# Four-layer graph network on one core: table parts and a convolution cut into steps, and the queues around layer 2's experts reordered

## The chip, the core and the metric

The kernel runs on one core of a Trainium2 chip, as one launch. The core has five engines that run on their own and meet only through semaphores: TensorE (PE, matrix products, its weight loads shown apart as PEld), VectorE (DVE), ScalarE (ACT), GpSimd (POOL) and SyncE (SP, which here only issues DMAs). Each takes its instructions strictly in its own order. The metric is the device time of one execution in microseconds, as the median of several runs; lower is better. Everything is computed in 32-bit floating point.

## The reference

1250 nodes with 512 features and 21250 edges pass through four layers. Every layer adds a graph convolution and an attention to the residual stream, and then a feed-forward part:

```
x = x + graph_l(norm(x)) + mix_l(norm(x));  x = x + ffn_l(norm(x))
layer 0: three GATv2 layers, h = relu(norm(segment_sum(xl[src] * alpha) + b + h))
         xl = h @ Wl[k], xr = h @ Wr[k]; alpha = segment softmax of leaky_relu(xl[src]+xr[dst]+ef) @ att[k]
layer 1: dense GAT and global attention; ffn: top-2 of experts plus shared part
layer 2: EGC: bases = x @ W_bases; agg = normalised neighbour sum of bases;
         conv[n,h,f] = sum_b w[n,h,b] * agg[n,b,f];  mix: linear attention
         ffn: xt = transpose(x); logits = conv1(gelu(conv3(xt)));  top 2 of 10 experts, elu
              sh = conv1(silu(conv9(xt)));  z = x + experts + sh;  norm(z) * g + b
layer 3: GCN: dinv = rsqrt(deg); out = segment_sum(h[row] * dinv[row]*ew*dinv[col]) + b
         mix: linear attention with q scaled;  ffn: top 2 of 32 experts with capacity
```

`conv9` and `conv3` are one-dimensional convolutions over the 1250 nodes, 9 and 3 taps wide.

## The kernel before

Nodes are cut into 10 tiles of 128 rows (`NT`), the last holding 98. Matrix products work on 128x128 weights and up to 512 columns. `psum(mm, tp, more)` deals out the eight PSUM banks by use; `evac` copies a PSUM result out, alternately on ACT and on DVE. The order of instructions on each engine is made by a scheduler at build time, from priorities in program order and modelled durations; inside `manual_schedule(engines=...)` the named engines keep the order in which the code is written. `experts` does that for SP. Stages run in this order (times are those of the profile):

- **Layer 0**, its ffn included, to 2240: preparation and linear attention to 320, then to 1620 the three GATv2 layers (`gatv2_fast`), edge tile by edge tile: rows of a left table are gathered by POOL (L231), PE expands the right table with one-hot matrices (L1280, L1281), DVE makes sum, and the score product `junk` (L1293, L1296), PE sums the weighted rows (L1347). While layer k runs, `gat_tables` makes the tables of layer k+1 (or, in `gat_first`, the first ones): for each node tile eight steps, four accumulating products for `wl` and four for `wr`, one step at a time between edge tiles, in a single PSUM bank, `tab`. With the fourth product of a half come ACT's copy (L1174, L1182) and a DVE operation on the same bank (L1176 `junk`, L1183).
- **Layer 1**, 2240 to 3160: dense attention, then experts from 2985 to 3103 and their tail.
- **Layer 2's attention** (`layer2_attn`), 3160 to 3397. From 3240 a loop over the ten tiles: a row of the count matrix `ct` is cast to `cs` by `evac`, ten products (L2571) give `y`, DVE scales it to `ag` (L2577), and for four bases b DVE makes `m = w[:, :, b] * ag[b]` (L2585), which POOL adds up. Linear attention (`q`, L748 to L817) runs between.
- **Layer 2's ffn** (`layer2_ffn`), 3397 to 3811. The normalised rows are transposed into `xp`; three sums and differences of even and odd columns (`form`, L2687) let a convolution be done with fewer products. Each weight `piece` is loaded in three DMAs and gets three sums on POOL (L2624 to L2626); up to five pieces are in flight. The 3-tap convolution gives the router's logits (3445 to 3513). Then follow, one after the other, the 9-tap convolution in two halves f of three pieces each (to 3622), the `second` products (L2780, L2782, to 3651), and 29 expert tiles (to 3811). For each, SP loads 256 KB of tokens `xe` and 1 MB of weights `w`, four buffers of each, three tiles ahead; PE transposes, multiplies (L2338), DVE and ACT make the elu (L2788 to L2792), PE multiplies again (L2343). The vector `be` is added to x by POOL during the transposes.
- **Layer 2's tail and the head of layer 3**, 3811 to 3919. `tail_steps` chains, tile by tile: two gathers of expert rows on POOL (`g`), z sums on DVE (L2807), row norm (ACT L2816, POOL L2817 with `ga`), the addition to x, the norm `xn` (L222), and the transposition `xnT` (PE L160 and `evac`). `layer3_attn` starts by making the degree scales `dinv` (L2837 to L2844) and writing them to memory and reading them back as `dinvb`, blocks of 107 nodes in columns (L2858 to L2863), 4 bytes at a time; it loads four 1 MB weights, scales `wq` on POOL (L762), and makes `o` on DVE (L2851), which ACT's queue writes out.
- **Layer 3**: GCN loop 3919 to 4225, then 32 experts to 4584.

Of the kernel before, what the change touches and what calls it, by code (L numbers as in the profile page):

```python
# [57 lines left out]
class Net:  # L58
# [675 lines left out]
    def linear_attention_steps(self, xn, xT, w_qkv, w_out, b_out, qscale, finish, added=None,  # L734
# [15 lines left out]
        with self.tc.tile_pool(name="la", bufs=1) as p, \  # L750
# [7 lines left out]
            for half in range(2):  # L758
                if half:
                    wq = self.weight(w_qkv[:, 0:D], 4, D)  # L760
                    if qscale != 1.0:
                        nc.gpsimd.tensor_scalar(wq, wq, qscale, None, op0=ALU.mult)  # L762
# [391 lines left out]
    def gat_tables(self, L, p, t, xT, bank):  # L1154
# [7 lines left out]
        def product(name, c):  # L1162
            def f():
# [4 lines left out]
                if c == 3:  # L1168
                    (left if name == "wl" else right)(d[name])
            return f  # L1170

        def left(m):
            o = p.tile([128, D + 1], F32, tag="tlo", name="tlo")
            nc.scalar.copy(o[:, :D], m)  # L1174
# [5 lines left out]
        def right(m):  # L1180
            o = p.tile([128, 2, D], F32R, tag="tro", name="tro")
            nc.scalar.copy(o[:, 0, :], m)  # L1182
# [3 lines left out]
        return [product(name, c) for name in ("wl", "wr") for c in range(4)]  # L1186
# [314 lines left out]
    def run(self, fast):  # L1501
# [4 lines left out]
        with self.tc.tile_pool(name="arm", bufs=1) as self.arm:  # L1506
# [23 lines left out]
            with self.psum():  # L1530
                self.layer2_ffn()
# [35 lines left out]
    def gat_first(self, pv, xtab):  # L1567
        nc, I = self.nc, self.I
        L = self.gat_vectors(0, pv)
        with self.tc.tile_pool(name="l0", bufs=1) as p, \  # L1570
# [3 lines left out]
            with self.tc.tile_pool(name="edge", bufs=1, side="right") as pe, \  # L1574
# [19 lines left out]
                def steps():  # L1594
                    for t in range(NT):
                        for i, f in enumerate(self.gat_tables(
# [3 lines left out]
                            if i % 4 == 3:  # L1600
# [710 lines left out]
    def experts(self, table, n, rowI, act):  # L2311
# [5 lines left out]
        with self.tc.tile_pool(name="ex", bufs=2) as p, \  # L2317
                self.tc.manual_schedule(engines={mybir.EngineType.SP}):
            def load(i):
                xe = p.tile([128, D], F32, tag="xe", name="xe", bufs=4)  # L2320
                nc.sync.dma_start(xe, self.rin[i * 128:(i + 1) * 128, :])
                row = nc.sync.value_load(rowI[0:1, i:i + 1], min_val=0, max_val=(n - 1) * 128)
                w = p.tile([128, 2050], F32, tag="w", name="w", bufs=4)
                nc.sync.dma_start(w, table[bass.ds(row, 128), :])
                return xe, w

            ahead = [load(i) for i in range(3)]
            for i in range(ntiles):
                xe, w = ahead.pop(0)
                if i + 3 < ntiles:  # L2330
                    ahead.append(load(i + 3))
# [16 lines left out]
                nc.scalar.dma_start(self.rout[i * 128:(i + 1) * 128, :], o)  # L2348

# [6 lines left out]
    def tail_steps(self, xn, xnT):  # L2356
# [5 lines left out]
        def turn(t):  # L2362
            self.transpose_tile(xnT[:, :, t * 128:(t + 1) * 128], xn[:, t, :])
# [11 lines left out]
        def need(t):  # L2375
            for u in range(t - n if t == 0 else t, t + 1):
                for i, f in enumerate(steps):
                    if 0 <= u + n - i < NT:
                        f(u + n - i)
# [104 lines left out]
    def layer2_attn(self):  # L2484
        nc, I = self.nc, self.I
        added = self.both_added()
        with self.tc.tile_pool(name="l2", bufs=1) as p:
# [17 lines left out]
            with self.tc.tile_pool(name="egc", bufs=2) as tmp, \  # L2505
# [55 lines left out]
                for t in range(NT):  # L2561
# [5 lines left out]
                    self.evac(cs, ct)  # L2567
# [604 lines left out]
```

## Time and profile before

| | |
|---|---|
| median of 3 runs | 4537.75 us (4534.72 to 4541.73) |
| profiled execution, its own time | 4585.94 us |
| its span | 4584.0 us |
| mean granted TensorE clock in it | 0.931 |
| PE, DVE, ACT, POOL busy, share of the span | 86%, 59%, 33%, 31% |
| GAT loop, 400 to 700: PE busy per 100 us | 89.25, 92.72, 93.80 |
| 3360 to 3440: PE busy per 20 us | 15.15, 9.87, 9.43, 12.82 |
| experts of layer 1, 2985 to 3103: PE busy, DMA | 112.59 of 118, 332 GB/s |
| experts of layer 2, 3651 to 3811: PE busy, DMA | 127.91 of 160, 252 GB/s |
| tail, 3800 to 3880: PE busy per 20 us | 9.52, 0.00, 12.41, 9.87 |

The profile records one execution, and every time below is on its clock, from the start of its span. An instruction is named by engine, source line and tile: `DVE m L2585` writes the tile m on VectorE. A busy time counts execution alone; what an engine waits for is put down to the instruction that released it last. The granted clock is the share of full speed that PE was given in a window. The profiled execution takes 48 us longer than the median.

### The profile page before, as it was taken

The page shows a single profiled execution, that of the slowest core. Times are in us where ns is not written, and L with a number is a line of the kernel's source. Part 1 is how long each engine was busy: PE and PEld are TensorE (multiplying, and loading weights), DVE is VectorE, ACT ScalarE, POOL GpSimd, SP SyncE. Part 2 cuts the span into 40 slices and gives each one's busy share as a digit, 9 for nine tenths or more (in the row PEclk, how much of TensorE's full clock was granted, in tenths as well). Part 3 has the DMA queues.
Part 4 walks back from the last instruction along what each step waited for, and adds up shares of the span by engine and source line. Part 5 has one row for each costly group of instructions (what it writes and reads, how often), then busy time and mean ns, then how long its engine had stood idle before and what let it go on. Part 6 is the DMA issues. An engine that isn't in the chain of part 4 may idle for free. (4 is left out here: it accounts for less than half of the span.)

```text
span 4584.0 us, 49281 instructions
## 1 busy us (share of the span) xinstructions
PE 3946.8 (86%) x15451; PEld 2434.6 (53%) x15466; DVE 2706.4 (59%) x6387; ACT 1502.9 (33%) x2738; POOL 1402.3 (31%) x1339
## 2 busy tenths in 40 slices
PE   6988998899788866799999999997969975898796
PEld 3435554555354444444788876564546552454474
DVE  5358784878398865533796767314692136587301
ACT  2213332334133354110364446122221122455121
POOL 2027662766366501102000000103253003676101
PEclk9989998999899978899999999999989997997798
DMA  6446664666466423401421110392012185565695
GB/s 221 150 123 199 184 188 138 192 185 187 130 180 189 145 66 105 121 18 59 147 68 42 44 41 21 140 336 80 12 54 71 69 282 154 162 205 170 244 338 188
DMA packets 283000, 647.57 MB, mean 141 GB/s; under 512 B 61673, under 2 KB 108905, under 8 KB 267322
## 3 DMA queue, kind: packets, MB, share of 16 engines
q1 hardware_dynamic: 169290, 357.13, 23.5%
q0 software_dynamic: 73088, 234.75, 17.9%
q10 hardware_dynamic: 40352, 52.44, 3.4%
q8 instruction: 127, 2.08, 0.2%
q14 instruction: 143, 1.17, 0.1%
HBM read 528.87 MB, written 120.65 MB: 142 GB/s over the span
## 5 line engine op out<-in xcount | busy, mean ns | idle before, releaser
L231 POOL DMA_INDIRECT xl<-xl,srcI x564 | 606.6, 1075 | 309.4 <-issue 137.4
L1347 PE MATMUL more<-xl,wT 128*128 128x512 f32 x1128 | 578.5, 600 | 26.8 <-ACT wT L1337 25.3
L1280 PE MATMUL mm<-hl,oh 121*128 121x512 f32 x564 | 419.6, 744 | 89.7 <-DVE s L1293 29.7
L1293 DVE TENSOR_TENSOR s<-xl,mm 128x512 f32<-128x512 f32 x534 | 355.0, 680 | 99.9 <-PE mm L1281 42.3
L1296 DVE SCALAR_TENSOR_TENSOR junk<-s,att 128x512 f32<-128x512 f32 x534 | 409.8, 767 | 6.2
L2099 PE MATMUL more<-hh,e 128*128 128x259 f32 x1600 | 384.0, 386 | 11.1 <-ACT o L2042 8.9
L2099 PEld LDWEIGHTS more<-hh,e 128*128 128x128 f32 x1600 | 295.0, 191 | 75.6 <-issue 16.0
L171 PE MATMUL mm<-w,xnT 128*128 128x512 f32 x640 | 307.7, 620 | 13.7 <-DVE xnT L136 5.3
L231 POOL DMA_INDIRECT g<-routed_out,getI x60 | 64.7, 1079 | 676.7 <-DMA routed_out<-o 490.0
L231 POOL DMA_INDIRECT hs<-gcn_h,srcI x188 | 215.5, 1146 | 96.5 <-issue 35.9
L1347 PEld LDWEIGHTS more<-xl,wT 128*128 128x128 f32 x1128 | 196.5, 192 | 86.2 <-ACT wT L1337 34.4
L1281 PE MATMUL mm<-hl,oh 121*128 121x512 f32 x564 | 238.2, 422 | 0.0
L1280 PEld LDWEIGHTS mm<-hl,oh 121*128 121x128 f32 x564 | 111.6, 198 | 232.6 <-issue 135.0
L2649 PE MATMUL mm<-form,cw 128*128 128x312 f32 (+1 forms) x640 | 181.2, 445 | 23.9 <-POOL cw L2626 10.5
L171 PEld LDWEIGHTS mm<-w,xnT 128*128 128x128 f32 x640 | 123.8, 198 | 141.6 <-issue 125.2
L2019 ACT ACTIVATE e<-r,hh 128x512 f32<-128x512 f32 (+1 forms) x240 | 154.2, 646 | 132.5 <-PE more L2099 121.5
L1267 ACT ACTIVATE oh<-nb 112x512 fp32r<-112x512 bf16 x141 | 88.5, 629 | 327.4 <-DMA nb<-nbt 232.9
L2925 PE MATMUL more<-hl,oh 128*128 128x512 f32 x376 | 166.3, 545 | 31.0 <-ACT hl L2885 11.2
L1166 PE MATMUL tab<-w,xT 128*128 128x512 f32 x320 | 165.1, 614 | 19.9 <-DVE junk L1176 18.1
L2022 ACT ACTIVATE e<-r,a 128x512 f32<-128x512 f32 (+1 forms) x240 | 152.3, 646 | 69.4 <-DVE e L2024 57.2
L2024 DVE TENSOR_TENSOR e<-e,e 128x512 f32<-128x512 f32 (+1 forms) x240 | 142.0, 598 | 51.5 <-ACT e L2019 45.1
L1281 PEld LDWEIGHTS mm<-hl,oh 121*128 121x128 f32 x564 | 113.1, 201 | 106.9 <-issue 105.4
(623 smaller groups left out, 7748.6 us busy)
## 6 DMA issues: line engine op xcount, KB each, us to landing
w<-L_ffn_Wp SPq DMA_DIRECT2D x64, 1024.0 KB
w<-L_ffn_table SPq DMA_DIRECT2D x56, 1025.0 KB
neg<-ntab SPq DMA_DIRECT2D x80, 320.0 KB
nb<-nbt SPq DMA_DIRECT2D x141, 128.0 KB
hl<-xr SPq DMA_DIRECT2D x36, 448.0 KB
xr<-tro SPq DMA_DIRECT2D x30, 512.0 KB
xe<-routed_in SPq DMA_DIRECT2D x56, 256.0 KB
routed_out<-o ACTq DMA_DIRECT2D x56, 256.0 KB
```

The source lines that it names most:

```text
L171: self.nc.tensor.matmul(p, lhsT=xT[:, c, t * 128:(t + 1) * 128], rhs=w[:, c, n0:n0 + n], start=c == 0, stop=c == k - 1)
L231: self.nc.gpsimd.indirect_dma_start(out=out, out_offset=None, in_=table, in_offset=bass.IndirectOffsetOnAxis(ap=idx, axis=0), bounds_check ...
L1166: nc.tensor.matmul(d[name], lhsT=xT(c), rhs=L[name][:, c, :], start=c == 0, stop=c == 3)
L1280: nc.tensor.matmul(m, lhsT=s, rhs=hl[:K, 0, :], start=True, stop=False)
L1281: nc.tensor.matmul(m, lhsT=s, rhs=hl[:K, 1, :], start=False, stop=not on_pe(i))
L1293: nc.vector.tensor_tensor(o, d["xl"][:, j, :D], s, op=ALU.add)
L1296: nc.vector.scalar_tensor_tensor(junk, s, 0.0, L["att"], op0=ALU.max, op1=ALU.mult, accum_out=d["lg"][:, j:j + 1])
L1347: nc.tensor.matmul(B[b]["y"], lhsT=d["wT"][:, j, :], rhs=d["xl"][:, j, :D], start=k == 0 and j == 0, stop=last and j == GE - 1)
L2019: nc.scalar.activation(e1[:, :n], R[q, k, 0][:, :n], AF.Exp, bias=HH[q][:, s, 256:257])
L2099: nc.tensor.matmul(ys[j], lhsT=e[:, j * 128:(j + 1) * 128], rhs=HH[q][:, s, :], start=s == 0, stop=s == NT - 1)
L2649: nc.tensor.matmul(m, lhsT=g[:, which, c, :], rhs=forms[form][:, c, q % 2, q // 2:q // 2 + n], start=j + c == 0, stop=j + 1 == len(gs) and ...
L2925: nc.tensor.matmul(y, lhsT=oh, rhs=hl[:, i], start=i + j == 0 and not (self.fast and k), stop=last and i + j == GE)
```

## The change

- `gat_tables` has ten steps per tile: ACT's copy stays with the fourth product, and the DVE operation with the table's write is a step of its own (`left`, `right`). `gat_first` yields at every fifth step instead of every fourth.
- `experts` loads its first weights before its first tokens, takes the number of buffers, and calls `beside(i)` after tile i.
- `tail_steps` keeps POOL in written order, in the tails of layers 1 and 2, and copies all of `xnT` on ACT.
- In `layer2_attn` the cast `cs` and the scaling `ag` go to ACT, and two of the four `m` become eight ACT operations of 128x64 each.
- `begin_convs` gives the convolution weights a pool of their own, three pieces instead of five, with one buffer for `g1`, loads the first piece before the ffn begins, and does the three sums on DVE. The transposes' copy into `xp` goes to ACT.
- The 9-tap convolution becomes a generator of steps in the two `more` banks: ten before the first expert tile of layer 2, two after each tile, none after tiles 7 to 9; `second` follows from tile 23 on, and the additions of the vector `be` with it. Layer 2's experts have three buffers, and PSUM there is 3 `mm`, 3 `tp`, 2 `more` banks.
- `gcn_scales` makes the degree scales and their way through memory at the start of the program order of `layer2_attn`; in the built program these instructions stand in layer 0, near 261 us of the profile. `wq` is scaled on ACT, and so is `o`.

```diff
                     wq = self.weight(w_qkv[:, 0:D], 4, D)
                     if qscale != 1.0:
-                        nc.gpsimd.tensor_scalar(wq, wq, qscale, None, op0=ALU.mult)
+                        nc.scalar.mul(wq, wq, qscale)
...
-                    (left if name == "wl" else right)(d[name])
+                    if name == "wl":
+                        o = p.tile([128, D + 1], F32, tag="tlo", name="tlo")
+                        nc.scalar.copy(o[:, :D], d[name])
+                    else:
+                        o = p.tile([128, 2, D], F32R, tag="tro", name="tro")
+                        nc.scalar.copy(o[:, 0, :], d[name])
+                    d[name] = d[name], o
             return f
-        def left(m):
-            o = p.tile([128, D + 1], F32, tag="tlo", name="tlo")
-            nc.scalar.copy(o[:, :D], m)
+        def left():
+            m, o = d["wl"]
             junk = p.tile([128, D], F32, tag="junk", name="junk", bufs=1)
             nc.vector.scalar_tensor_tensor(junk, m, 0.25, L["att"], op0=ALU.mult,
                                            op1=ALU.mult, accum_out=o[:, D:])
             nc.sync.dma_start(L["tl"][ts, :], o)
-        def right(m):
-            o = p.tile([128, 2, D], F32R, tag="tro", name="tro")
-            nc.scalar.copy(o[:, 0, :], m)
+        def right():
+            m, o = d["wr"]
             nc.vector.tensor_tensor(o[:, 1, :], m, o[:, 0, :].bitcast(F32), op=ALU.subtract)
             nc.sync.dma_start(L["tr"][ts], o.bitcast(F32))
-        return [product(name, c) for name in ("wl", "wr") for c in range(4)]
+        return ([product("wl", c) for c in range(4)] + [left] +
+                [product("wr", c) for c in range(4)] + [right])
...
-            with self.psum():
+            with self.psum(3, 3, 2):
...
-                            if i % 4 == 3:
+                            if i % 5 == 4:
...
-    def experts(self, table, n, rowI, act):
+    def experts(self, table, n, rowI, act, bufs=4, beside=None):
...
+            def weights(i):
+                row = nc.sync.value_load(rowI[0:1, i:i + 1], min_val=0, max_val=(n - 1) * 128)
+                w = p.tile([128, 2050], F32, tag="w", name="w", bufs=bufs)
+                nc.sync.dma_start(w, table[bass.ds(row, 128), :])
+                return w
+            def tokens(i):
+                xe = p.tile([128, D], F32, tag="xe", name="xe", bufs=bufs)
                 nc.sync.dma_start(xe, self.rin[i * 128:(i + 1) * 128, :])
-                row = nc.sync.value_load(rowI[0:1, i:i + 1], min_val=0, max_val=(n - 1) * 128)
-                w = p.tile([128, 2050], F32, tag="w", name="w", bufs=4)
-                nc.sync.dma_start(w, table[bass.ds(row, 128), :])
-                return xe, w
-            ahead = [load(i) for i in range(3)]
+                return xe
+            ws = [weights(i) for i in range(bufs - 1)]
+            xes = [tokens(i) for i in range(bufs - 1)]
+            if beside is not None:
+                beside(-1)
             for i in range(ntiles):
-                xe, w = ahead.pop(0)
-                if i + 3 < ntiles:
-                    ahead.append(load(i + 3))
+                xe, w = xes.pop(0), ws.pop(0)
+                if i + bufs - 1 < ntiles:
+                    ws.append(weights(i + bufs - 1))
+                    xes.append(tokens(i + bufs - 1))
...
+                if beside is not None:
+                    beside(i)
...
-            for u in range(t - n if t == 0 else t, t + 1):
-                for i, f in enumerate(steps):
-                    if 0 <= u + n - i < NT:
-                        f(u + n - i)
+            with self.tc.manual_schedule(engines={mybir.EngineType.Pool}):
+                for u in range(t - n if t == 0 else t, t + 1):
+                    for i, f in enumerate(steps):
+                        if 0 <= u + n - i < NT:
...
-                    self.evac(cs, ct)
+                    nc.scalar.copy(cs, ct)
...
-                    nc.vector.tensor_scalar(af, y[:, :256], dinv[:, t:t + 1], None,
-                                            op0=ALU.mult)
+                    nc.scalar.activation(af, y[:, :256], AF.Copy, scale=dinv[:, t:t + 1])
...
-                        nc.vector.tensor_tensor(
-                            m, wt[:, :, b:b + 1].to_broadcast([128, 8, 64]),
-                            ag[:, b:b + 1, :].to_broadcast([128, 8, 64]), op=ALU.mult)
+                        if b < 2:
+                            nc.vector.tensor_tensor(
+                                m, wt[:, :, b:b + 1].to_broadcast([128, 8, 64]),
+                                ag[:, b:b + 1, :].to_broadcast([128, 8, 64]), op=ALU.mult)
+                        else:
+                            for h in range(8):
+                                nc.scalar.activation(m[:, h, :], ag[:, b, :], AF.Copy,
+                                                     scale=wt[:, h, b:b + 1])
...
+        cw = self.convs.enter_context(self.tc.tile_pool(name="l2cw", bufs=3, side="right"))
...
+            g = piece_tile()
+            g1 = cw.tile([128, 4, 128], F32, tag="g1", name="g1", bufs=1)
+            for i, dst in ((0, g[:, 0]), (2, g[:, 3]), (1, g1)):
+                k = 4 * (3 * j + i)
+                nc.sync.dma_start(dst, src[f][:, k:k + 4, :])
+            nc.vector.tensor_tensor(g[:, 1], g[:, 0], g[:, 3], op=ALU.add)
+            nc.vector.tensor_tensor(g[:, 2], g[:, 1], g1, op=ALU.subtract)
+            nc.vector.tensor_tensor(g[:, 1], g[:, 1], g1, op=ALU.add)
+            G[src.tensor.name, f, j] = g
...
-                        nc.gpsimd.tensor_tensor(self.x[:r, t, :], self.x[:r, t, :], be[:r],
-                                                op=ALU.add)
...
+                def shared():
...
+                        yield from conv(sh1, f, 0, 9, silu, self.more)
...
+                def second(t):
                     ts = slice(t * 128, (t + 1) * 128)
+                    g = last[0]
                     y = self.mm()
                     for f in range(2):
-                        nc.tensor.matmul(y, lhsT=sh[:, f, ts], rhs=ws[:, f, :],
+                        nc.tensor.matmul(y, lhsT=sh[:, f, ts], rhs=g[:, f, :],
                                          start=f == 0, stop=False)
-                    nc.tensor.matmul(y, lhsT=gT[:, ts], rhs=b2, start=False, stop=True)
+                    nc.tensor.matmul(y, lhsT=gT[:, ts], rhs=g[:11, 2], start=False, stop=True)
                     nc.vector.tensor_tensor(z[:, t, :], z[:, t, :], y, op=ALU.add)
+                    r = rows(t)
+                    nc.gpsimd.tensor_tensor(self.x[:r, t, :], self.x[:r, t, :], g[:r, 3],
+                                            op=ALU.add)
+                steps = shared()
+                left = list(range(NT))
+                def beside(i):
+                    for _ in range(10 if i < 0 else 0 if 7 <= i < 10 else 2):
+                        if next(steps, self) is self and left and i >= 23:
+                            second(left.pop(0))
...
+                self.experts(I["L2_ffn_table"], 10, rowI, elu, 3, beside)
+                for _ in steps:
+                    pass
+                for t in left:
+                    second(t)
+            self.convs.close()
...
+        deg = self.s4[:, :, 3]
...
+        nc.scalar.activation(dinv, dinv, AF.Sqrt)
...
+            dtab = self.dram.tile([NB * BN], F32, name="dinv")
+            nc.sync.dma_start(dtab[:NP].rearrange("(t p) -> p t", p=128), dinv)
+            dinvb = self.dinvb = p.tile([BN, NB], F32, name="dinvb")
+            r = NP - (NB - 1) * BN
+            nc.sync.dma_start(dinvb[:, :NB - 1], dtab[:(NB - 1) * BN]
+                              .rearrange("(b p) -> p b", p=BN))
+            nc.sync.dma_start(dinvb[:r, NB - 1:], dtab[(NB - 1) * BN:NP]
+                              .rearrange("(b p) -> p b", p=r))
...
-                nc.vector.tensor_scalar(o, self.nat(xnT, w, t), dinv[:, t:t + 1], None,
-                                        op0=ALU.mult)
+                nc.scalar.activation(o, self.nat(xnT, w, t), AF.Copy, scale=dinv[:, t:t + 1])
```

## Prediction

> **What bounds the kernel now.** Four views, coarse to fine. First the page's busy shares:
>
> ```profile
> PE 3946.8 (86%) x15451; PEld 2434.6 (53%) x15466; DVE 2706.4 (59%) x6387; ACT 1502.9 (33%) x2738; POOL 1402.3 (31%) x1339
> ```
>
> TensorE (PE) is the pace-setter on average, and the change removes none of its matmuls. So it can only gain where PE stands idle, 637 us in all. The second view, busy time in chosen windows, says where that is. Columns: window, length, then busy us of PE, its weight loads, DVE, ACT, POOL; granted clock; DMA share; GB/s.
>
> ```profile
> 600.00:700.00 100.00, 93.80 (x347) 53.94 (x346) 84.52 (x223) 41.78 (x75) 63.22 (x66) 1.00 0.63 181
> ...
> 3380.00:3400.00 20.00, 9.87 (x30) 5.61 (x29) 18.84 (x44) 2.32 (x8) 6.08 (x4) 0.74 0.16 49
> 3400.00:3420.00 20.00, 9.43 (x33) 7.29 (x32) 20.00 (x28) 2.73 (x5) 19.18 (x7) 0.59 0.32 109
> ...
> 3651.00:3811.00 160.00, 127.91 (x698) 90.90 (x696) 54.44 (x145) 46.59 (x146) 0.00 (x0) 0.96 0.75 252
> ...
> 3820.00:3840.00 20.00, 0.00 (x0) 0.00 (x0) 10.05 (x24) 1.76 (x5) 10.40 (x10) 0.50 0.93 198
> ```
>
> Row 1 is the GAT loop: PE nearly full. Rows 2 and 3, the end of layer 2's attention and the front of its ffn: PE half idle, DVE full. Row 4, layer 2's experts: DVE and ACT a third busy, PE waiting for transfers. Row 5, the tail: PE silent, DMA engines occupied but moving only 198 GB/s. The third view, waits by releaser (total us, times, longest), names the waits; the first two from 380 to 1240, the others from 3240 to 3812:
>
> ```profile
> DVE junk L1176 <- ACT tlo L1174: 97.4, 20, 9.1
> PE tab L1166 <- DVE junk L1176: 18.1, 16, 1.4
> PE tp L160 <- DVE q L817: 13.2, 5, 4.5
> PE tp L160 <- DVE xp L2675: 10.1, 1, 10.1
> PE mm L2649 <- POOL cw L2626: 10.5, 1, 10.5
> PE tp L160 <- DMA xe<-routed_in: 27.6, 19, 3.2
> ```
>
> The fourth is used below. A sum is made against the profiled execution, 4585.94 us; the median of the runs shown is 48 us less, and a gain is carried over unchanged.
>
> **1. Table parts in ten steps (380 to 1240).** DVE stands 97.4 us at L1176 for ACT's copy, 20 times, with the edge tile's work queued behind it. In the changed order PE's last wl product comes two edge tiles (each about 2 us here: one m, one s, one junk) earlier in PE's queue, ACT's copy one group earlier in ACT's, and the junk keeps its place on DVE, so the wait of 4.9 us a time should nearly go. No operation is added; the wr half keeps its place. But DVE idle is not PE idle: what PE loses behind DVE in these windows is 18.1 on L1176 itself, 12.9 on lg, 9.3 and 5.2 on s and junk, 3.7 on m: 49 us. Bounds 0 (all of it comes back as another wait) and 40; I take **20**, because PE has only 6 to 12 us idle per 100 there, some of it short handshakes.
>
> **2. Layer 2's attention loop (3240 to 3397).**
>
> ```profile
> L2585 DVE TENSOR_TENSOR m<-comb,ag 128x512 f32<-128x512 f32 x40 | 42.2, 1060 | 2.7 <-POOL out L2588 2.6
> L136 DVE CAST cs<-ct 128x1280 fp32r<-128x1280 uint16 x8 | 6.4, 803 | 0.0
> ```
>
> DVE loses 20 m (21.2), 8 casts (6.4), 10 ag (4.8): 32 us of about 150. Per tile PE has 14.4 (143.8 busy over ten), DVE falls from about 14 to 10. All of it lands on ACT: 16 products of 128x64 per tile, one cast, one ag, one copy. No such small product with a per-row factor is in the trace. The nearest row is the experts' `r<-mm,w` 128x128 with a per-row bias, 0.368 us, the next ACT instruction starting 0.26 after it; 64 columns less at 0.83 ns (128 columns 0.302, 512 columns 0.622) give 0.31 alone, 0.21 in sequence. **Here a rule speaks against the change**: the Trainium skill, "ScalarE: Activation LUTs", Rules for kernel authors, says multiplications belong on VectorE, not ScalarE; its section on the cost of a table load puts 279 ns before the first element, 0.33 us for one of these and 0.24 in sequence. By the row 16 cost 3.4 to 5.0 us, by the page 3.8 to 5.3. DVE did the same two in 2.1 (1.4 uncontended). The rule is right on price and doesn't decide: ACT has 5.0 us per tile now (its rows of this window sum to 50 over ten) and, with cast 1.25, ag 0.4, copy 0.58, 10.6 to 12.5 afterwards, under PE's 14.4. It would decide from 0.5 us each. What goes is PE's 13.2 on q and a share of DVE's backlog that fills 3360 to 3420.
>
> **3. Front of the convolution (3397 to 3513).** PE waits 10.1 for xp (a memset queued late on DVE), 6.0 for forms, 10.5 for POOL's cw. The three sums per piece go from POOL (1.3 to 8 us beside DVE's forms) to DVE (0.69 each by the nearest tensor_tensor row, 8 us for four pieces), ten x+=be (11.9 us POOL) go into the experts. The same DVE sums now stand in DVE's queue, so they may hold forms instead. Steps 2 and 3 together: PE idle in 3360 to 3440 is 4.9+10.1+10.6+7.2 = 33, plus 8 in the six windows before and 3 in the next; I take **27**, between 12 (DVE stays full to 3420) and 38.
>
> **4. Shared convolution beside the experts (3513 to 3811).** Before, in a row: convolution 109, `second` 29, experts 160 = 298. PE work in it: 192 matmuls at 0.566 = 109, 29, and 128, so 266 if nothing waits: the most to win is 32. Against it: (a) f=1's three pieces (2.3 MB) are issued by SP only after w(12), with g1 single-buffered, and PE has both expert tile 10's second product and DVE its next m behind them: three landings of about 5 us, less the one tile of 4.4 that covers, 10 to 13, I take **11**; SP's w(13) waits meanwhile, two tiles ahead, hidden. (b) Three tiles without steps, about 4. (c) Start, two thin tiles, last tile: 6. (d) Silu and Exp alternate on ACT: 12 table loads where there were two. The row is ACT_TABLE_LOAD 1.28 us, 13 in all; the same section of the skill adds a 1.38 us drain, 2.66 a switch, 27 in all. Conv products between cover most either way; I charge 3 by the row, and 10 by the page at the low end. Weight buffers fall from 4 to 3 (two ahead): with 9 us of PE per tile against 1.28 MB at 250 GB/s = 5.1 us, hidden. 32-11-4-6-3 = **8**, from -12 to 22. The `second` adds on DVE and POOL are hidden: POOL is idle there.
>
> **5. Layer 2's tail (3811 to 3919).** SP's issues, then POOL's scaling:
>
> ```profile
> 3828.52 0.30 SPq L2861 DMA_DIRECT2D dinvb<-dinv  x1
> 3828.86 16.59 SPq L2863 DMA_DIRECT2D dinvb<-dinv  x1
> 3845.49 0.58 SPq L141 DMA_DIRECT2D w<-L_mix_w_qkvT  x1
> ...
> 3856.47 5.51 POOL L762 TENSOR_SCALAR w<-w 128x2048 f32<-128x2048 f32 x1 [9.41 <-PE tp L160]
> ```
>
> Four-byte transfers hold SP for 27 us and the DMA engines at 0.93 while the gathers land 5 us apart. All go to layer 0. POOL's 9.41 wait and 5.51 in front of z*ga ended in PE's longest later stall, 9.3 on xn at 3872. The scaling is now ACT's: 0.622 + 1536 x 0.83 ns = 1.9 us. But it is second in ACT's queue, and needs the fourth 1 MB weight: 4.2 MB from about 3814 at 200 to 230 GB/s (the later pair, 2.1 MB, took from 3845.5 to about 3856) and shared with gathers, it lands at 3832 to 3840, and the first z scaling (3836.05 before, PE starts 3846.35) stands behind it. So the start wins 0 to 5 and can lose 2. Copies and o on ACT take DVE from 6.3 to 5.2 us per tile. Together **+11**, from -5 to 25. Layer 1's tail, same POOL order with no POOL wait before: **+2**. Layer 1's experts, weights before tokens: **+2**.
>
> **6. Degrees early (about 260).** SP's blocked 27 us come behind mtab; the edge-attribute loads queued there slip from 275 to about 300, and are needed at 313. **-2**, from 0 to -15.
>
> Sum: 20+27+8+11+2+2-2 = 68. 4585.94-68 = 4518; median **4470**.
>
> **Rivals.**
> *A, small gain, 0.20.* DVE's idle in GAT returns as other waits (8), ACT's queue behind wq eats the tail (-3), experts break even (0), front 18: about 23, **4515**. For it: PE is already at 94 in GAT, and the head of line on ACT is real. Against: the front's 33 us idle has named causes, all removed.
> *B, large gain, 0.14.* The upper ends of 1, 2+3, 4 and 5 with 3 for the rest: 35+36+20+20+3 = 114, **4424**. For it: four stages each with a named stall. Against: the piece stall in step 4.
> *C, slower, 0.06.* In 3513 to 3811 the steps don't fill the waits but add to them: PE, DVE and ACT each take orders in sequence, so an expert's exchange (product, m, Exp, hT) waits behind conv sums, Silu and table switches. Price: 298 + 16 for pieces + 27 for switches + 29 tiles at 1.5 for two buffers ahead (44) = 385, or 87 lost; with 60 won elsewhere 27 slower: **4565**. It decides from 358, 12.3 us per expert tile. Against: both engines are a third busy, and two to four conv products stand between an expert's two products.
> *D, the change does not do what it says, 0.03:* gains cancel, **4538**.
>
> **How the numbers follow.** The forecast has 0.57 with 4440 to 4500 as its own range. A measurement of this kernel can't tell less than 0.2%, 9 us, from no change. Faster: forecast, A and B = 0.57+0.20+0.14, less a little of A = 0.90; same 0.04; slower 0.06. The range runs from B's to A's, 4420 to 4525.
>
> **What would show it.** L1176's wait on ACT under 20 us (step 1), with PE above 95 per 100. DVE m x20, PE no more than 5 idle per 20 in the windows that were 3360 to 3420. One stall of 10 us on `more` for cw at expert tile 10; the stretch from router to tail under 295. No SP issue over 1 us in the tail, first product earlier than 35 us after the last expert. Wrong if ACT passes 14 us per tile in step 2, if PE waits for ACT's z behind wq, or if layer 0 starts its edges late.

## The result

| | kernel before | changed kernel |
|---|---|---|
| median, 4 runs each | 4539.74 us (4534.72 to 4552.93) | 4478.57 us (4474.11 to 4483.65) |
| ratio, 95% interval | | 0.9858 (0.9838 to 0.9878) |
| profiled execution, its span | 4585.94, 4584.0 | 4474.11, 4472.3 |

61 us faster by the medians: 9 us above the forecast of 4470, and inside the range of 4420 to 4525. The two profiled executions differ by 112 us, which is more. The profiled execution of the kernel before took 48 us more than its median; the first experiment finds a chip on which that kernel takes about so long in all of its runs, so a slower chip is the likely reason, though the chip of the first profile is not on record. So a stage is compared below with the same stage on a like chip where there is one, and a kernel with the kernel before by its ratio.

### The profile after

Page of the changed kernel, part 1:

```profile
PE 3913.2 (87%) x15451; PEld 2422.1 (54%) x15466; DVE 2696.8 (60%) x6357; ACT 1598.2 (36%) x2955; POOL 1358.0 (30%) x1308
```

As many matmuls as before; ACT is 95 us busier, DVE only 10 us less. Windows of the changed kernel (same columns as before): the GAT loop, the end of layer 2's attention, the front of its ffn, the wait before its experts, the convolution with the experts, the tail.

```profile
600.00:700.00 100.00, 96.93 (x356) 55.89 (x355) 91.64 (x230) 42.08 (x76) 65.25 (x65) 1.00 0.61 178
3320.00:3340.00 20.00, 9.34 (x25) 4.80 (x24) 15.94 (x36) 8.38 (x27) 7.34 (x5) 0.76 0.08 27
3340.00:3360.00 20.00, 13.50 (x58) 10.46 (x57) 19.84 (x39) 5.33 (x11) 0.00 (x0) 0.78 0.27 93
3460.00:3480.00 20.00, 9.98 (x40) 7.01 (x39) 0.48 (x1) 1.01 (x2) 11.78 (x12) 0.80 0.70 266
3434.00:3721.00 287.00, 260.31 (x1164) 174.98 (x1163) 89.59 (x244) 75.62 (x176) 32.17 (x30) 0.96 0.57 193
3720.00:3740.00 20.00, 1.18 (x3) 0.35 (x2) 7.33 (x15) 3.40 (x3) 6.37 (x6) 0.61 0.77 268
```

PE is busy for 97 us of 100 in this window of the GAT loop, where it was 94; the half-idle stretch between attention and convolution is two windows long instead of four; the tail moves 268 GB/s instead of 198 but PE is silent there as before. The waits of the changed kernel (the first two from 380 to 1240, the others from 3190 to 3722):

```profile
DVE junk L1182 <- ACT tlo L1171: 41.1, 6, 9.2
...
PE tab L1166 <- DVE junk L1182: 2.8, 2, 1.4
...
PE tp L160 <- DMA xe<-routed_in: 21.4, 7, 10.0
PE tp L2726 <- DVE x L185: 10.7, 1, 10.7
PE tp L160 <- DVE q L817: 9.6, 6, 2.3
PE mm L2688 <- DVE form L2735: 6.5, 1, 6.5
...
PE more L2688 <- DVE cw L2646: 0.6, 1, 0.6
```

20 waits of DVE for ACT's copy have become 6, though 41 us are left where I expected under 20. The waits for xp and for POOL's sums are gone. Those for tokens are 7 instead of 19, but in sum only 21.4 us instead of 27.6, since one of 10.0 for the first tokens is new. New is also a wait of PE for one DVE addition to x (10.7). The prediction had neither at that size.

### The profile page after: what moved, and what is told of

It is laid out like the page before. It is cut to its first block, busy times and chain, and to the rows that moved or that the text cites. A ratio compares the mean times of both kernels' runs of the same rounds, so it can differ in the third digit from the quotient of the medians.

```text
span 4472.3 us, 49493 instructions
## 1 busy us (share of the span) xinstructions
PE 3913.2 (87%) x15451; PEld 2422.1 (54%) x15466; DVE 2696.8 (60%) x6357; ACT 1598.2 (36%) x2955; POOL 1358.0 (30%) x1308
## 4 chain that ended last, share of the span: by engine, by line
PE 31%; DVE 8%; DMA 5%; issue 4%; ACT 2%; POOL 2%; SPq 0%; POOLq 0%; ACTq 0%; DVEq 0%
PE more L2105 5%; PE mm L1968 4%; PE mm L179 3%; PE mm L171 3%; PE mm L3168 2%; PE mm L2357 2%; PE mm L2352 2%; PE more L2688 2%; DMA hs<-gcn_h,srcI 1%; PE mm L2688 1%; PE mm L2067 1%; DMA xe<-routed_in 1%; PE mm L776 1%; DVE junk L1996 1%; DVE e L2030 1%
## 5 line engine op out<-in xcount | busy, mean ns | idle before, releaser
L231 POOL DMA_INDIRECT xl<-xl,srcI x564 | 617.5, 1095 | 282.4 <-issue 134.6
L1299 DVE TENSOR_TENSOR s<-xl,mm 128x512 f32<-128x512 f32 x534 | 357.7, 679 | 79.0 <-PE mm L1287 64.4
L2966 ACT ACTIVATE hl<-hs,rec 128x512 fp32r<-128x512 f32 x188 | 131.0, 717 | 98.2 <-DMA hs<-gcn_h,srcI 45.7
```

The lines of the kernel that those rows point to most:

```text
L231: self.nc.gpsimd.indirect_dma_start(out=out, out_offset=None, in_=table, in_offset=bass.IndirectOffsetOnAxis(ap=idx, axis=0), bounds_check ...
L1299: nc.vector.tensor_tensor(o, d["xl"][:, j, :D], s, op=ALU.add)
```

## The experiments

Stage lengths, in us, from landmarks of PE in the profiles: "GAT k" is from first to last weighted-row product (`more<-xl,wT`) of that layer; "front" from the attention loop's first product to the 9-tap convolution; "experts" from there to the last expert product of layer 2; "tail" to the first GCN product. Each row is one profiled execution.

| kernel | start to GAT 0 | GAT 0 | between | GAT 1 | between | front | experts | tail | GCN |
|---|---|---|---|---|---|---|---|---|---|
| before | 372.4 | 378.0 | 77.0 | 371.2 | 76.4 | 266.3 | 300.1 | 112.6 | 301.6 |
| before_again | 370.6 | 379.2 | 73.6 | 375.7 | 73.1 | 269.9 | 301.4 | 113.5 | 296.9 |
| tables_only | 373.4 | 362.4 | 70.7 | 358.7 | 75.5 | 271.0 | 303.8 | 115.9 | 295.7 |
| serial_conv | 377.6 | 364.5 | 64.3 | 365.1 | 73.8 | 241.9 | 308.5 | 99.5 | 300.9 |
| m_on_dve | 382.6 | 362.5 | 72.9 | 358.3 | 71.1 | 251.1 | 288.6 | 100.9 | 300.3 |
| changed | 376.2 | 362.1 | 63.8 | 357.3 | 59.7 | 243.7 | 286.8 | 100.6 | 289.6 |
| after_again | 376.7 | 362.2 | 64.1 | 357.5 | 59.7 | 244.6 | 288.8 | 98.3 | 290.6 |
| scales_mid | 369.5 | 363.3 | 63.9 | 359.8 | 59.9 | 244.5 | 288.0 | 98.0 | 290.1 |
| pre16 | 376.8 | 362.1 | 64.6 | 358.7 | 58.2 | 244.0 | 284.8 | 94.1 | 293.3 |
| wq_pool | 375.0 | 361.7 | 63.1 | 359.6 | 56.1 | 244.2 | 286.5 | 101.2 | 286.1 |
| best | 372.1 | 365.6 | 65.8 | 361.4 | 59.4 | 245.2 | 284.5 | 97.3 | 291.6 |
| best_mdve | 370.4 | 363.5 | 64.2 | 360.3 | 60.1 | 251.3 | 284.1 | 94.9 | 288.5 |
| sums_pool | 377.6 | 362.0 | 64.4 | 357.6 | 59.5 | 247.9 | 287.0 | 100.3 | 289.3 |
| tail_free | 377.6 | 363.3 | 65.0 | 361.3 | 58.9 | 244.6 | 285.8 | 99.3 | 291.5 |

before_again to m_on_dve ran on one chip, where the kernel before took 4589.47 (11 runs, 4571.9 to 4603.15); after_again to wq_pool on another, with 4542.70; the last four on a third, with 4542.66. The chips of the rows "before" and "changed" are not on record.

**before_again**: the kernel before, profiled once more.

> The kernel before, unchanged, profiled once more. The profiled pair differs by 111.8 us (4585.94 against 4474.11), the medians by 61. By stages the pair gives 59.5 us to the three GAT layers (first to last weighted-row product, 1245.1 to 1185.6), 12 to layer 3's GCN loop, which the change does not touch (301.6 to 289.6), and about 40 to the rest. Theory: the first profile of before had a slow 40 to 50 us in gather-heavy stages; this one then has a GAT stretch near 1205, a GCN loop near 290, and its own time within 15 us of 4540. Rival: the GAT gain of 59 is real; then the GAT stretch is again 1240 or more.

4589.34, on a chip where the kernel before has a median of 4589.47: GAT stretch 1243.3, GCN loop 296.9. The theory as written fell: the profile of before was no odd execution, it repeats. The rival's number came true, its reading did not: of the 59.5 us between the GAT stretches of the first pair, the two pauses between layers give 30, and these are 71 to 76 on this chip (but for one of 64.3 in serial_conv) and 56 to 66 on the two others, whatever the kernel. GAT 0 and 1 differ by 30 with the kernel, not with the chip. So about 48 of the 112 us between the first two profiles are put down to the chip.

**tables_only**: the kernel before with the new `gat_tables` and nothing else.

```diff
...
-        return [product(name, c) for name in ("wl", "wr") for c in range(4)]
+        return ([product("wl", c) for c in range(4)] + [left] +
+                [product("wr", c) for c in range(4)] + [right])
...
```

> The kernel before with only the table parts in ten steps (and the yield at every fifth). Theory (my step 1, 20 us): 4520, ratio 0.9955, between 0.993 and 0.998. Rival 1 (the profiled pair is right): 55 to 60 us, ratio 0.987. Rival 2 (idle time of DVE that PE never waited for): within 5 us of before, ratio above 0.999.

4555.52, ratio 0.9933 (0.9909 to 0.9957): 31 to 34 us, and GAT 0 and 1 are 33.8 shorter than in before_again on the same chip. Between my 20 and the rival's 55. PE's waits in GAT 0 and 1, first in before_again (371 to 1199):

```profile
PE tab L1166 <- DVE junk L1176: 17.1, 15, 1.9
PE more L1347 <- ACT wT L1337: 14.2, 11, 2.1
...
PE tp L1305 <- DVE lg L1302: 13.6, 12, 3.5
```

then in tables_only (373 to 1165):

```profile
PE tp L1311 <- DVE lg L1308: 13.8, 12, 3.7
PE tab L1166 <- ACT xT L1415: 6.6, 4, 2.2
...
PE more L1353 <- ACT wT L1343: 3.7, 4, 1.4
...
PE tab L1166 <- DVE junk L1182: 1.4, 1, 1.4
```

The wait on junk goes, and most of that on ACT's wT, which I had not counted. The wait on lg, which I had counted as won in part, stays, and one on ACT's xT grows from 1.2 to 6.6. Why wT comes earlier is open. It did not stand behind the copies of the tables in ACT's queue: of the 11 waits in before_again, ten are for a wT right behind the operation `oh` and none for one right behind such a copy. One of them in ACT's queue:

```profile
530.01 0.63 ACT L1267 ACTIVATE oh<-nb 112x512 fp32r<-112x512 bf16 x1 [3.23 <-DMA nb<-nbt]
530.55 0.57 ACT L1337 COPY wT<-tp 128x512 f32<-128x512 f32 x1
```

The load of nb that ended this idle time had been issued at 523.85, when DVE's `m` (L1309) released its buffer. So a late DVE may reach PE by way of SP and ACT; no run separates that. The two loops' sums of busy time, from the windows of the two loops in before_again and in tables_only:

```profile
sum 754.00, PE 706.02 PEld 396.04 DVE 581.79 ACT 286.60 POOL 442.60; mean PE 353.01 PEld 198.02 DVE 290.90 ACT 143.30 POOL 221.30
```

```profile
sum 720.00, PE 694.76 PEld 394.05 DVE 602.25 ACT 287.24 POOL 448.25; mean PE 347.38 PEld 197.03 DVE 301.13 ACT 143.62 POOL 224.13
```

Of 34 us, PE's idle time gives 23 (48 to 25); the other 11 is busy time of the same matmuls (2480 recorded against 2485); a matmul's end is modelled, so how this part splits is less sure than the sum. The granted clock reads 0.99 in both loops of before_again and 1.00 in both of tables_only; 1% of 706 us is 7, so the clock can be a part of the 11.

**serial_conv**: the changed kernel, convolution and `second` ahead of the experts.

```diff
-                    for _ in range(10 if i < 0 else 0 if 7 <= i < 10 else 2):
-                        if next(steps, self) is self and left and i >= 23:
-                            second(left.pop(0))
+                    if i < 0:
+                        for _ in steps:
+                            pass
+                        while left:
+                            second(left.pop(0))
```

> The changed kernel with all steps of the 9-tap convolution and all second products ahead of the first expert tile, as in the kernel before; three expert buffers and all else as changed. From the start of this convolution to the last expert product the pair shows 300.1 before and 286.9 after. Theory: the interleaving is worth that 13 us, so 4492, ratio 0.989. Rival: the steps only move stalls (the 10 us wait for tokens at the start and the thin tiles eat what is won), and serial is no slower: 0.986.

4527.89, ratio 0.9867 (0.9843 to 0.9890). The interval holds both answers. The stage tells them apart: 308.5 against 288.6 in m_on_dve, on the same chip and with the changed kernel's code there. So the interleaving is worth 20 us of the stage. The waits for tokens explain 6 of them: they are back at 28.2 us (19 times), but m_on_dve still has 22.5 (7 times). PE is idle for 39.7 us of this stage against 28.0, and its recorded busy time is 268.8 against 260.6. The serial stage is also 7 longer than that of before_again (301.4), which has four expert buffers and loads tokens first; what costs these 7 was not taken apart.

**m_on_dve** and **best_mdve**: four m on VectorE, the first against the changed kernel, the second against `best`.

```diff
-                        if b < 2:
+                        if b < 4:
```

> The changed kernel with all four m per tile on VectorE again (160 small ScalarE products less). Theory: DVE limits this stage, 20 m at about 0.8 to 1.06 us come back, of which PE feels half: about 10 us slower, 4489, ratio 0.988. Rival: the contention with GpSimd only moved from m to the q and x operations (q 979 to 1513 ns, x 680 to 1141 ns on the mean), so the split is worth nothing: 0.986 or lower.

> The same kernel with all four m of a tile on VectorE. The first run without the split had a ratio of 0.9844, no worse than with it, while its stage from the loop to the 9-tap convolution read 251.1 us against 244.6. Theory (stages): the split is worth 6 us, so 0.0014 above the run beside it. Rival (totals): it is worth nothing or costs up to 5, ratio equal or lower. The stage reading should repeat: 6 us longer from the loop's first product to the 9-tap convolution.

m_on_dve: 4519.70, ratio 0.9844 (0.9820 to 0.9868); best_mdve: 4482.33, 0.9863 (0.9848 to 0.9878), beside `best` at 0.9832 on the same chip. The totals point opposite ways, so they can't carry a 6 us question. The front does: 251.3 without the split and 245.2 with it on that chip; 251.1 in m_on_dve, against 244.6 in after_again on another chip and 241.9 in serial_conv on the chip of m_on_dve. The split is worth 6 us, or 9 by that last pair. Its mechanism is in VectorE's groups, of best_mdve and then of best, in the loop (3188 to 3325):

```profile
L2608 DVE TENSOR_TENSOR m<-comb,ag 128x512 f32<-128x512 f32 x32 | 36.0, 1133 | 0.0
L817 DVE TENSOR_TENSOR q<-q,den 128x512 f32<-128x512 f32 x9 | 8.7, 964 | 0.0
```

```profile
L2608 DVE TENSOR_TENSOR m<-comb,ag 128x512 f32<-128x512 f32 x17 | 14.4, 845 | 0.0
L817 DVE TENSOR_TENSOR q<-q,den 128x512 f32<-128x512 f32 x9 | 14.0, 1559 | 0.0
```

15 m less are 21.6 us less, but the q operations grow by 5.3. Taken one by one in best_mdve, the 8 m with GpSimd idle for at least 80% of their time last 692 ns at most, the other 24 last 1283 in the mean; in best 11 of the 17 m have GpSimd idle. Of the nine q eight run beside a busy GpSimd in both kernels, for 999 ns and then 1667 in the mean. So a part of what slowed m falls on q instead. The rival's mechanism is real, and takes a quarter of the 21.6.

**after_again**: the changed kernel once more, beside its variants.

> The changed kernel, unchanged, profiled and timed beside its variants on one chip. The chip of the last four runs took 4589 for the kernel before, 50 us more than the chip of the first medians, so absolute times don't compare between calls. Theory: the ratio holds, 0.986, and the profile's GAT stretch and GCN loop differ from the first profile of the changed kernel if the chip is a slow one (GCN loop 300 instead of 290).

4479.23, ratio 0.9855 (0.9834 to 0.9876); GCN loop 290.6. The ratio holds on another chip.

**scales_mid**: the degree scales' tiles in a pool that opens after layer 1's attention.

```diff
+            with self.tc.tile_pool(name="deg", bufs=1) as self.deg:
...
-        nc, p = self.nc, self.arm
+        nc, p = self.nc, self.deg
```

> The changed kernel with the tiles of the degree scales in a pool that opens after layer 1's attention, which moves their round trip from layer 0 into layer 1's dense attention, where the DMA engines are at 0.13. Theory: in the changed kernel SP is held 13 us near 263 and 7 at 276, the edge-attribute loads go out 9 us later than before and PE waits 9.8 for oh, so this gives back 4 to 6 us: ratio 0.0010 lower than that of the changed kernel beside it. Rival: the start of the edges is set by something else (the transposes before it), and nothing changes.

4474.33, ratio 0.9850 (0.9828 to 0.9873): in total not to be told from the changed kernel. The start is 7.2 shorter (369.5 against 376.7). SP in the changed kernel:

```profile
263.27 0.37 SPq L2916 DMA_DIRECT2D dinv<-dinv  x1
276.19 0.26 SPq L2919 DMA_DIRECT2D dinvb<-dinv  x1
276.50 7.10 SPq L2921 DMA_DIRECT2D dinvb<-dinv  x1
283.70 0.94 SPq L628 DMA_DIRECT2D eat<-hi  x2
```

and in scales_mid:

```profile
275.20 0.79 SPq L628 DMA_DIRECT2D eat<-hi  x2
```

The edge attributes go out 8.5 us earlier. PE still waits 10.0 for them (`oh<-eat`; 9.8 in the changed kernel), but it did so in the kernel before too (10.3 at the same place, put down to nb). The wait that the round trip adds stands before that one. In the changed kernel, PE's wait for the edge data `fields`, and DVE's for the gather `mg` that goes into them:

```profile
PE tp L523 <- DVE fields L621: 9.5, 1, 9.5
```

```profile
277.99 1.28 DVE L620 TENSOR_TENSOR mg<-mg,loops 48x512 f32<-48x512 f32 x2 [9.02 <-DMA mg<-mtab,meanI]
```

The same two in scales_mid:

```profile
PE tp L523 <- DVE fields L621: 4.3, 1, 4.3
```

```profile
272.59 1.29 DVE L620 TENSOR_TENSOR mg<-mg,loops 48x512 f32<-48x512 f32 x2 [4.02 <-DMA mg<-mtab,meanI]
```

In the kernel before PE's wait is 4.2. GpSimd issues the gather at 269.26 in the changed kernel and at 269.14 in scales_mid, so beside the scales' write of 4-byte elements it lands 5 us later; and the edge data are late before SP's queue holds them up. The read-back stands at 2668 in scales_mid and holds SP for 7.25.

**pre16**: 16 steps before the first expert tile.

```diff
-                    for _ in range(10 if i < 0 else 0 if 7 <= i < 10 else 2):
-                        if next(steps, self) is self and left and i >= 23:
+                    for _ in range(16 if i < 0 else 0 if 4 <= i < 7 else 2):
+                        if next(steps, self) is self and left and i >= 20:
```

> The changed kernel with 16 instead of 10 convolution steps before the first expert tile, the pause at tiles 4 to 6 instead of 7 to 9, and the second products from tile 20. The profile of the changed kernel shows one wait of 10.0 us for the first tokens, with PE idle, which the prediction had at 3. Theory: six more steps of 2.3 us cover it, 8 us gained, ratio 0.0018 lower than that of the changed kernel. Rival: the step total is the same and the tiles freed at the end run at the DMA's pace instead, so at most 3 us.

4471.71, ratio 0.9842 (0.9819 to 0.9866), experts 284.8 against 288.8, tail 94.1 against 98.3. By the medians that is 7.5 us, near what I expected, though the intervals overlap. The reason is not mine: PE's wait in pre16 is still there.

```profile
PE tp L160 <- DMA xe<-routed_in: 9.0, 1, 9.0
```

The scheduler put only four more records of convolution products ahead of the first transposition (72 in the last stretch instead of 68); the rest went between the first expert tiles. What holds the tokens is GpSimd's queue of scatters, in the changed kernel from 3449.59 on, 1.29 us apart:

```profile
3449.59 1.12 POOL L239 DMA_INDIRECT routed_in<-z,putI  x1 [85.35 <-DVE slot L2301]
3451.02 1.00 POOL L239 DMA_INDIRECT routed_in<-z,putI  x1 [0.30 <-issue]
```

Twenty of them take 26 us, and the token loads are issued at 3476.82. In the kernel before, the whole convolution stood beside them.

**wq_pool**: wq scaled on GpSimd.

```diff
-                        nc.scalar.mul(wq, wq, qscale)
+                        nc.gpsimd.tensor_scalar(wq, wq, qscale, None, op0=ALU.mult)
```

> The changed kernel with wq scaled on GpSimd again (5.5 us there instead of 1.9 on ScalarE), all else as changed. Theory: GpSimd's written order puts it behind the tail's gathers or between them, and PE's 9.3 us wait for xn comes back in part: 5 us slower, ratio 0.001 higher. Rival: with the weights there before the expert end, it finds a free place before the first gathers and costs nothing, or it even helps ScalarE's first z: 0 to -2 us.

4474.00, ratio 0.9855 (0.9833 to 0.9877), tail 101.2 against 98.3. In its trace:

```profile
3736.39 5.42 POOL L762 TENSOR_SCALAR w<-w 128x2048 f32<-128x2048 f32 x1
```

It runs between the sixth gather and the first z*ga, where GpSimd has nothing to do. In total it makes no difference, 3 us of the tail at most: the engine of this multiplication never was the point.

**best**: scales_mid and pre16 together.

> The changed kernel with both improvements at once: the degree scales' round trip in layer 1's dense attention, and 16 convolution steps before the first expert tile. Theory: they touch different stages, so 5 and 7 us add, ratio 0.983. If the single gains were scatter (each was within its interval), 0.9855.

4465.50, ratio 0.9832 (0.9818 to 0.9845), against 0.9855 (0.9834 to 0.9876) for the changed kernel in after_again: alone the two read 0.0005 and 0.0013 below it, together 0.0023. They add by their centres; the intervals overlap. It has the lowest ratio of this study. Its profiled execution, 4485.71, is the slowest of its five.

**sums_pool**: the pieces' sums on GpSimd.

```diff
-            nc.vector.tensor_tensor(g[:, 1], g[:, 0], g[:, 3], op=ALU.add)
+            nc.gpsimd.tensor_tensor(g[:, 1], g[:, 0], g[:, 3], op=ALU.add)
...
```

and the same for the other two.

> The changed kernel with the three sums of each convolution piece on GpSimd again, where they waited and took 1.3 to 8 us before. Theory (my step 3): PE's 10.5 us wait for cw is what this part removed; with additions of the vector be gone from GpSimd too, half returns: 5 us longer from the loop's end to the 9-tap convolution, ratio 0.987. Rival: with forms earlier and three pieces only, GpSimd is idle there and VectorE is the limit (its x at L185 holds PE 10.7 us), so VectorE freed of 8 us makes it 3 us faster.

4489.87, ratio 0.9887 (0.9872 to 0.9902), against 0.9855 (0.9834 to 0.9876) for the changed kernel in after_again. The front is 247.9, 3.3 longer, so some 11 us of the difference in the medians lie elsewhere; the profiled execution, 4480.20, is the fastest of its four and can't show them. They are not explained. PE in this kernel, in the front:

```profile
PE mm L2688 <- POOL cw L2645: 12.9, 1, 12.9
```

The wait is back as foretold, but it takes the place of the one for VectorE's forms (6.5 in the changed kernel, 0.4 here).

**tail_free**: GpSimd in the scheduler's order in the tails.

```diff
-            with self.tc.manual_schedule(engines={mybir.EngineType.Pool}):
...
```

> The changed kernel with GpSimd in the scheduler's order in the tails, as before the change; copies and scalings stay on ScalarE. The tail of layer 2 (last expert product to first GCN product) reads 112.6 and 113.5 us before, 98 to 101 after. Theory: the round trip gone from SP and copies on ScalarE bring most of it, so this is 103 to 105, ratio 0.9865. Rival: GpSimd's order is the larger part: 108 or more, ratio 0.9875.

4481.64, ratio 0.9862 (0.9847 to 0.9877), tail 99.3. Neither came: with the written order the tail is 98.3 and 100.6, so the order is worth 1 us at most.

## Why the prediction was right

The forecast was 68 us less, 4470; 61 was measured. Each named stage gained, but the sum came out so near by luck: step 1 gained more than its term, layer 1 and the start lost. And the parts below, read from single profiles and partly across chips, come to 67 to 79, so 6 to 18 us of loss were not found.

- **Step 1, table parts, 20: mis-sized, 34 measured.** That DVE's idle time would go and only a part of it come back to PE was right: PE's idle time fell by 23. But it came from other waits than I counted: 15.7 from junk and 10.5 from ACT's wT, which I had left out, and nothing from lg. The term that failed is PE's busy time, which I held fixed because no matmul goes: it fell by 11. DVE's own wait did not fall under 20 either.
- **Steps 2 and 3, the front, 27: 25.3** (before_again 269.9, after_again 244.6 on another chip; serial_conv, on the first one, 241.9). The split of m is worth 6, the sums' move to VectorE 3. The other 16, of ACT's copies and cast, the earlier memset and be's move, were not taken apart. DVE still sets the pace between loop and convolution, now with `x L185` holding PE for 10.7: two windows have 10.7 and 6.5 us idle, where I expected 5 at most. ACT has 9.8 us of work per tile (97.66 in 3190 to 3340), a little under my 10.6 to 12.5. For the price of the small products the estimate from the skill was the better one. ACT's group in the changed kernel (3190 to 3340):

```profile
L2612 ACT ACTIVATE m<-ag,comb 128x64 f32<-128x64 f32 x160 | 39.9, 334 | 24.7 <-POOL out L2614 24.7
```

  334 ns alone and 39.9/160 = 0.25 us in sequence, where my estimate from the Trainium skill ("ScalarE: Activation LUTs", What ACT_TABLE_LOAD costs) was 0.33 and 0.24 and that from my row 0.31 and 0.21. Its rule (Rules for kernel authors) that a multiplication belongs on VectorE did not decide: in 3300 to 3400 of the kernel before, VectorE was busy for 93.48 us and ScalarE for 28.31.
- **Step 4, experts, 8: 13** (300.1 and 301.4 before, 286.8 and 288.8 after; PE idle there 36 and 26.7). The interleaving alone is worth 20; 7 are lost to the rest of the change in this stage, for which I had no term. The piece stall of 11 was too high: PE waits 0.6 for cw itself and 3.7 at most for a token held up behind the pieces, and stands idle 7.8 in 3520 to 3560. The start, charged in the 6 of item (c), was too low: 10.0 for the first tokens, because all 109 us of convolution stood between the router and the tokens before, and ten steps do now. Of item (d), ACT in 3434 to 3721 of the changed kernel:

```profile
L2818 ACT ACT_TABLE_LOAD x7 | 9.0, 1283 | 4.6 <-DVE y L2712 4.5
L2861 ACT ACT_TABLE_LOAD x7 | 9.0, 1283 | 0.1
```

  With one more these are 15 loads where there were 3. The next ACT instruction starts about 0.01 us after each, so nothing is seen of the 1.38 us drain that I had charged at the low end, and PE waits for ACT only 0.5 us in this stage and for hT, which comes by way of ACT, 3.9 (4.1 before): my 3 was too high as well.
- **Step 5, tail, 11: 12 to 15.** Its parts were wrong. I feared ACT behind wq with weights landing at 3832 to 3840, 21 to 29 after the last expert product. SP and ACT in the changed kernel:

```profile
3716.60 0.39 SPq L141 DMA_DIRECT2D w<-L_gnn_W  x1
3717.04 1.77 SPq L141 DMA_DIRECT2D w<-L_mix_w_qkvT  x3
```

```profile
3737.79 1.91 ACT L762 ACTIVATE w<-w 128x2048 f32<-128x2048 f32 x1 [0.19 <-DMA g<-routed_out,getI]
```

  The weights go out 4.6 before the experts end (3721.18), and the multiplication runs 16.6 after it, in the 1.9 us of my sum, with no one waiting. wq's engine and GpSimd's order, which I had as parts of the gain, are worth 3 and 1 at most. What is left is the round trip gone from SP and the copies on ScalarE; PE starts 27.6 after the end instead of 35.2. A kernel with the round trip back in the tail was not tried, so this rests on the trace. It is not all gain: 4 MB of weights are now issued before the last expert rows land (DVE waits 6.2 for them, 2.2 before), and the first gather is issued 7.7 after the end, not 3.6.
- **Layer 1, +4: not seen.** Its experts take 116 in the two profiles of before and 120 to 126 in every other, tables_only included, whose code there is that of before; from their end to layer 2's attention loop it is 142 before and 143 after. The cause stays open.
- **Step 6, degrees early, -2: -4 to -7.** The edge-attribute loads slip as foretold, from 274.93 to 283.70. What I left out is the gather `mg` ahead of them, which lands 5 us later beside the scales' write; PE's wait for `fields` grows by as much.

Rival A fell with tables_only and the front, B with the front, the experts and the tail, C with serial_conv: with the steps between the tiles the stage is 20 shorter, not longer.

## What to carry to other kernels

A wait can reach TensorE by way of several queues, so count TensorE's waits for all engines, not only for the one that the change frees. Compare waits by their sum: 7 instead of 19 waits for tokens were 21.4 us instead of 27.6. Before a stretch of work is moved to fill idle time, ask what it covered where it was: here it covered 26 us of scatters. A stage of 300 us read by landmarks settles a 6 us question that 4500 us of total time leaves open, if both profiles are of like chips.

## What was unexpected of the hardware

- Chips differ by stage. The kernel before took 4589 on one and 4543 on two others, with 9 to 11 runs on each. It shows in the pauses between GAT layers (71 to 76, but for one of 64.3, against 56 to 66) and the GCN loop (296 to 302 against 286 to 293), stages in which rows are gathered; dense attention (629 to 631) and layer 3's experts (240 to 241) are alike.
- The same 4-byte read-back held SP for 16.59 us beside gathers and weights, and for 7.10 in layer 0. The write before it is not free there either: a gather issued at the same time as without it landed 5 us later.
- A DVE operation that is taken away beside GpSimd's additions does not take its slowness along: m fell from 1133 to 845 ns, q rose from 964 to 1559.
